# Folding the second layer's attention weights between the steps of the first layer

## The chip, the cores and the metric

The kernel runs on one core of one Trainium2 chip. The metric is the time of one execution on the device in microseconds (us), as the median over runs. All data are 32-bit floats. In the trace every such matmul appears as two instructions ("passes"), and every transpose on TensorE as one.

## The reference

Two layers are computed on x of shape (4, 512, 512). Each adds an attention part and a feed-forward part to x, both computed from the normed rows xn:

```
xn = layernorm(x);  x = x + attn0(xn) + ffn0(xn)
xn = layernorm(x);  x = x + attn1(xn) + ffn1(xn)
```

`attn0` has 32 heads of 16 channels. It walks the 512 tokens in 32 steps of 16; each step uses the state (W1, b1) that the step before left:

```
Z1   = xk @ W1 + b1
grad = backward of a norm at Z1, against the target xv - xk
out  = xq + norm(xq @ W1 - (eta * tril(xq xk^T)) @ grad + b1 - tril(eta) @ grad)
W1   = W1 - (last_eta * xk)^T @ grad;   b1 = b1 - sum(last_eta * grad)
```

Then a norm over the 512 channels and a product with `o_w` follow. `ffn0` is a gated feed-forward with 1408 inner channels.

`attn1` has 16 heads of 128 channels and works from latents, 128 wide for keys and values and 384 for queries:

```
c_kv = xn @ W_DKV + b_DKV;   k = c_kv @ W_UK + b_UK;   v = c_kv @ W_UV + b_UV
c_q  = xn @ W_DQ  + b_DQ;    q = c_q  @ W_UQ + b_UQ
first 64 channels of each head: q <- rope(q @ W_QR), k <- rope(k @ W_KR), the second half of them zero
out  = softmax(q k^T / sqrt(128)) @ v @ W_O + b_O
```

The weights allow two products ahead of any token: a head's columns of W_UK and W_UQ by W_KR and W_QR (the "rotated" columns, 64 per head), and a head's W_UV by its rows of W_O (the "value-output" product, 128 x 512 per head). Since softmax's rows sum to one, the value bias goes to the output as the constant row b_UV @ W_O, which can be added to b_O. `ffn1` has four experts; token i belongs to expert i mod 4.

## The kernel before

**Stages.** Three blocks follow one another in the code: the first layer with the second layer's latents (line 90 on), the second layer's experts (line 822 on), the second layer's attention heads (from about line 928). Each opens memory pools of its own, in SBUF and in PSUM (eight banks).

**The first layer.** Tokens are cut into 8 chunks of 64 per sequence; a chunk has four steps. The loop over n (line 773) emits for each step the state product (`first_product`), the gradient on VectorE (`gradient`), the update of the state, which is kept in PSUM (`update`), and the output (`emit_out`). These depend on each other from step to step. Everything else is "work": a chain of generators, one per chunk (`between`, line 650), that holds the feed-forward (`gate_up` for 11 blocks, `down` for two halves of the rows with 11 weight tiles each), the next chunk's normed and transposed input, its keys, values and queries, and the end of the chunk before (`finish`: norm of the outputs over heads, norm over channels, product with `o_w`, the second layer's layernorm, transposed rows stored to `xe_d`). The last chunk's work ends with `latents`: the products with W_DKV and W_DQ, from rows read back from `xe_d`, stored to `lat_d`.

Each generator yields a number after each piece, its cost in us as the author counts it. `fill(us)` (line 698) adds us to a balance and emits pieces until it is used up. A step calls it three times, with `GAPS` (`LAST_GAPS` in the last chunk): before `update`, before `emit_out`, and after it. A chunk's first step waits in the program until that chunk's inputs are emitted (`done`). After the last step `LAST_FINISH` alternates fills with the pieces of the last `finish`, and what is left follows.

The order on an engine is not exactly this one. When the program is compiled, a list scheduler places the instructions with this order as their priority, and passes over those that it takes not to be ready. The chip then runs each engine's and each DMA queue's instructions in that fixed order. SyncE (SP) issues nearly all loads, in order; ScalarE issues some stores between its own instructions.

**Buffers.** A pool gives each tag so many slots. Those that matter here: `wd` (4 slots, 128 x 512), through which the tiles of the down weights come; `sg` (2); `pn_rs` (1); `xs` (2), through which the latents are stored; `xT` and `q1` (3 each); and in PSUM `pj` (2 banks), which serves nearly every product of the stage other than feed-forward and step (`psum()`, line 102).

**The value bias.** `value_bias(hg)` (line 522) runs in chunks 1 to 4, one head group (4 heads) each. It loads the four heads' rows of W_O as `wd` tiles, multiplies each by its bias spread over 32 columns into one quarter of a PSUM bank, copies the bank, multiplies it by a constant 1/32 to sum it and adds it to `bo`.

**The experts.** Per expert, four pairs of gate and up products (`pg`, `pu`), then four down products (`po`), from one PSUM pool of 2 banks for each of its four tags.

**The heads.** `group_weights(hg)` (line 942) loads a group's weights and folds them. Each 128 x 512 block is transposed per head on TensorE (`turned`, line 933), copied by ScalarE, multiplied by `wkr` or `wqr` and copied over the first 64 channels of each head (`fold`, line 951). Value weights are transposed likewise and multiplied by the output weights into `vo`. Group 0 is folded at the start of the stage, the next one each time sequence 1 of a group begins. A head of a sequence (64 in all) then takes key and query products (`pk`, `pq`), rotation on VectorE and GpSimd, scores (`sc`), softmax on ScalarE and VectorE, a transpose of the probabilities by 16 DMAs from SyncE (`prT`), the context (`pc`) three heads behind, and per four heads the output (`po`).

Of the kernel before, what the change touches and what calls it, by code (L numbers as in the profile page):

```python
# [12 lines left out]
F32 = mybir.dt.float32  # L13
# [23 lines left out]
GAPS, LAST_GAPS = (11.0, 4.0, 8.0), (10.0, 4.0, 5.0)  # L37
LAST_FINISH = (9.0, 17.0, 5.0)
# [17 lines left out]
def trunk_kernel(ctx: ExitStack, tc: tile.TileContext, a: dict, out: bass.AP):  # L56
# [15 lines left out]
    xe_d = dram.tile([2 * NCHUNK, P, NC, E, 32], F32, tag="xe_d", name="xe_d")  # L72
    lat_d = dram.tile([1 + QC // P, P, B, NCHUNK, CT], F32, tag="lat_d", name="lat_d")
# [15 lines left out]
    with ExitStack() as px:  # L89
# [47 lines left out]
        def norm_turn(ch):  # L137
            xTs[ch] = wk.tile([P, NC, CW], F32, tag="xT", name=f"xT{ch}", bufs=3)
            for u in range(2):
                nc.scalar.copy(xTs[ch][:, :, u * P : (u + 1) * P], transposed(xns.pop((ch, u))))  # L140
                yield 0.6
# [96 lines left out]
        def queries(ch):  # L238
            return features(ch, wq_w, q1, "q1", 3)
# [275 lines left out]
        ones32 = one.tile([P, P], F32, tag="ones32", name="ones32")  # L515
        nc.vector.memset(ones32, 1.0 / 32)
        buv16 = one.tile([H, D], F32, tag="buv16", name="buv16")
        nc.gpsimd.dma_start(out=buv16, in_=a["b_UV"].rearrange("(h d) -> h d", d=D))
        buv_b = one.tile([P, H, 32], F32, tag="buv_b", name="buv_b")
        nc.gpsimd.dma_start(out=bo, in_=a["b_O"].unsqueeze(0).to_broadcast([P, HS]))  # L520

        def value_bias(hg):
            if hg == 0:
                pt = psum()[:, :H]
                nc.tensor.transpose(pt, buv16, ident[:H, :H])
                nc.vector.tensor_copy(buv_b, pt.unsqueeze(2).to_broadcast([P, H, 32]))
            pb = psum()
            for h, r in enumerate(quarters):
                w = wk.tile([P, HS], F32, tag="wd", name=f"wob_{hg}_{h}", bufs=4)
                nc.sync.dma_start(out=w, in_=a["W_O"][(4 * hg + h) * D : (4 * hg + h + 1) * D, :])  # L530
                mm(pb[r], buv_b[:, 4 * hg + h, :], w)
            part = wk.tile([P, HS], F32, tag="xt", name=f"bo_part{hg}", bufs=4)
            nc.vector.tensor_copy(part, pb)
            yield 1.3
            pb = psum()
            mm(pb, ones32, part)
            nc.vector.tensor_add(bo, pb, bo)
            yield 0.86
# [7 lines left out]
        def finish(ch):  # L546
# [45 lines left out]
            if ch >= NCHUNK - 2:  # L592
                t = wk.tile([P, NC, CW], F32, tag="xT", name=f"xl_{ch}", bufs=3)
# [56 lines left out]
        def between(ch):  # L650
# [12 lines left out]
            extra = value_bias(ch - 1) if 1 <= ch <= NHG else iter(())  # L663
# [13 lines left out]
            yield from extra  # L677
# [14 lines left out]

        done = {0}
# [83 lines left out]
        for n in range(NM):  # L777
# [8 lines left out]
            update(n, g, pre)  # L786
            fill(gaps[1])
            emit_out(n, po, gh)
            fill(gaps[2])
# [420 lines left out]
```

## Time and profile before

| | |
|---|---|
| median of 3 runs | 2160.28 us (2159.66 to 2162.85) |
| the profiled execution | 2162.4 us |
| its span, first to last instruction | 2160.6 us |
| busy: TensorE, its weight loads | 2068.6 us (96%), 1181.5 us (55%) |
| busy: VectorE, ScalarE, GpSimd | 1177.5, 883.3, 504.9 us |
| first expert matmul, last one ended, first fold of a head group | 1022.4, 1191.9, 1192.75 us |
| matmuls of the folds: transposes, rotations, value-output | 80, 128 and 32 instructions |

How to read it: all times are us from the first instruction of one profiled execution. PE is TensorE, PEld its weight loads, DVE is VectorE, ACT ScalarE, POOL GpSimd, SP SyncE; SPq and ACTq are the DMA issues of those engines. In a row of the timeline, the first number is the start and the second the length of a run of like instructions; in brackets stands the time that the engine was idle before it, and what released it. `out<-in` are tiles by their names in the code. TensorE matmuls overlap, so the distance from start to start tells what one costs, and its listed length is longer.

### The profile page before, as it was taken

The numbers are of one execution on the slowest core, as the hardware profiler recorded it, in microseconds if no ns is written. First come the engines' busy times: TensorE is split into PE (matmuls) and PEld (weight loads), VectorE is DVE, ScalarE is ACT, GpSimd is POOL, SyncE is SP. The second block draws the span as 40 slices with busy tenths as digits, with TensorE's granted clock in tenths as the row PEclk, the third lists the DMA queues.
The fourth block names the chain that finished last, engine by engine and source line by source line (L and its number), as shares of the span: only waits on it lengthen the run. The fifth ranks groups of instructions, "written<-read, shape, count | busy, mean of one in ns | idle before, by whom it ended". The sixth has DMA issues, their size and how long they took to land.

```text
span 2160.6 us, 29279 instructions
## 1 busy us (share of the span) xinstructions
PE 2068.6 (96%) x10050; PEld 1181.5 (55%) x10050; DVE 1177.5 (54%) x2384; ACT 883.3 (41%) x1805; POOL 504.9 (23%) x555
## 2 busy tenths in 40 slices
PE   8999999999999999995999899999999999999998
PEld 6776676767676767543444444444444444444444
DVE  4445656465656565631111556664666656666663
ACT  2334353434434343332000454444544545455552
POOL 4233233233333333301001211110111111111110
PEclk9999999999999999998999989999999999999999
DMA  6556364646474646526610233333233333333332
GB/s 179 153 138 190 112 193 134 180 135 175 131 197 129 173 136 192 171 75 235 226 59 25 89 92 77 74 94 75 76 77 93 75 72 78 75 75 75 95 94 76
DMA packets 286960, 259.27 MB, mean 120 GB/s; under 512 B 52956, under 2 KB 210845, under 8 KB 285789
## 3 DMA queue, kind: packets, MB, share of 16 engines
q1 hardware_dynamic: 272752, 245.96, 41.0%
q10 hardware_dynamic: 11500, 5.32, 0.9%
q0 software_dynamic: 2560, 6.13, 0.8%
q8 instruction: 81, 1.33, 0.3%
q14 instruction: 67, 0.54, 0.1%
HBM read 161.60 MB, written 29.62 MB: 89 GB/s over the span
## 4 chain that ended last, share of the span: by engine, by line
PE 75%; DVE 10%; ACT 9%; DMA 3%; issue 2%; POOL 1%; SPq 0%; ACTq 0%; DVEq 0%; POOLq 0%
PE pj L100 14%; PE pf L100 11%; PE po L1069 10%; PE pc L1054 7%; PE sc L1008 5%; PE pq L999 5%; PE pd L100 5%; ACT prob L1013 3%; PE epg L855 3%; PE epo L900 3%; PE epu L855 3%; ACT prob L1015 2%; PE pso L100 2%; PE pk L992 2%; PE pz L100 2%
## 5 line engine op out<-in xcount | busy, mean ns | idle before, releaser
L1008 PE MATMUL sc<-kT,qT 96*128 96x512 f32 x512 | 235.7, 598 | 15.1 <-ACT prob L1013 13.5
L985 POOL TENSOR_TENSOR kT<-t_k,t_k 32x512 f32<-32x512 f32 x64 | 80.7, 1261 | 717.9 <-PE pq L999 403.3
L1013 ACT ACTIVATE prob<-sc,mx 128x512 f32<-128x512 f32 x256 | 173.1, 683 | 147.1 <-DVE mx L1010 147.1
L1069 PE MATMUL po<-vo,ctxT 128*128 128x512 f32 x512 | 223.0, 593 | 1.5 <-ACT ctxT L1059 1.5
L1054 PE MATMUL pc<-prT,lv 128*128 128x512 f32 x496 | 224.0, 594 | 0.0
L1023 DVE STREAM_TRANSPOSE tt<-prob 128x512 f32<-128x512 f32 x252 | 166.6, 697 | 60.3 <-ACT prob L1015 56.7
L100 PE MATMUL pf<-xT,wg 128*128 128x256 f32 x704 | 171.8, 385 | 4.2 <-DVE hid L459 3.9
L999 PE MATMUL pq<-cq,uq 128*128 128x512 f32 x384 | 175.2, 592 | 0.0
L1015 ACT ACTIVATE prob<-prob,sm 128x512 f32<-128x512 f32 x256 | 171.7, 724 | 3.6 <-DVE sm L1014 3.6
L1008 PEld LDWEIGHTS sc<-kT,qT 96*128 96x128 f32 x512 | 96.0, 191 | 140.9 <-issue 110.6
L100 PE MATMUL pf<-xT,wu 128*128 128x256 f32 x704 | 168.0, 380 | 0.5 <-DMA wu<-in_wu 0.3
L1010 DVE TENSOR_REDUCE mx<-sc 128x1 f32<-128x512 f32 x256 | 164.4, 681 | 7.0 <-PE sc L1008 4.4
L100 PE MATMUL pd<-wd,hid 128*128 128x512 f32 x352 | 165.2, 600 | 0.2
L1069 PEld LDWEIGHTS po<-vo,ctxT 128*128 128x128 f32 x512 | 97.1, 190 | 124.1 <-issue 116.2
L1054 PEld LDWEIGHTS pc<-prT,lv 128*128 128x128 f32 x496 | 94.5, 191 | 120.0 <-issue 112.1
L100 PEld LDWEIGHTS pf<-xT,wg 128*128 128x128 f32 x704 | 131.0, 190 | 32.1 <-DVE hid L459 6.7
L100 PEld LDWEIGHTS pf<-xT,wu 128*128 128x128 f32 x704 | 133.2, 190 | 22.1 <-issue 2.6
L1079 DVE TENSOR_TENSOR y<-po,y 128x512 f32<-128x512 f32 x64 | 44.2, 691 | 152.5 <-PE po L1069 152.5
L993 ACT ACTIVATE kT<-pk,b_UK 64x512 f32<-64x512 f32 x64 | 43.7, 683 | 196.7 <-PE pk L992 196.7
L999 PEld LDWEIGHTS pq<-cq,uq 128*128 128x128 f32 x384 | 73.0, 190 | 91.8 <-issue 86.8
L459 DVE SCALAR_TENSOR_TENSOR hid<-pf,us,sg 128x256 f32<-128x256 f32 x88 | 41.5, 474 | 132.6 <-ACT sg L458 132.0
L297 POOL TENSOR_SCALAR sk<-k,m 128x256 f32<-128x256 f32 x64 | 61.3, 969 | 158.1 <-PE pz L100 158.1
(256 smaller groups left out, 3151.8 us busy)
## 6 DMA issues: line engine op xcount, KB each, us to landing
prT<-tt SPq DMA_DIRECT2D x1008, 64.0 KB, 2.0
wd<-in_wd SPq DMA_DIRECT2D x176, 256.0 KB, 3.0
wg<-in_wg SPq DMA_DIRECT2D x88, 256.0 KB, 3.5
wu<-in_wu SPq DMA_DIRECT2D x88, 256.0 KB, 3.4
rows<-rows SPq DMA_DIRECT2D x128, 66.0 KB, 2.2
kv<-rows SPq DMA_DIRECT2D x32, 264.0 KB, 4.4
gu<-in_gu SPq DMA_DIRECT2D x3, 2048.0 KB, 8.7
xt<-in_x SPq DMA_DIRECT2D x32, 128.0 KB, 3.2
```

The source lines that it names most:

```text
L100: nc.tensor.matmul(out, lhsT=lhsT, rhs=rhs, start=start, stop=stop, skip_group_check=True)
L855: nc.tensor.matmul(ps, lhsT=w[:, c, col : col + P], rhs=xe[:, :, c, e, :], start=(c == 0), stop=(c == NC - 1))
L900: nc.tensor.matmul(po, lhsT=inter[:, i, b * P : (b + 1) * P], rhs=dn[:, i, :], start=(i == 0), stop=(i == EI // P - 1),)
L985: nc.gpsimd.tensor_sub(t[RD:mid, :], t1[RD:mid, :], t2[RD:mid, :])
L999: nc.tensor.matmul(pq, lhsT=w["uq"][i][:, h, :], rhs=cq[:, i, b, :], start=(i == 0), stop=(i == nq - 1))
L1008: nc.tensor.matmul(ps, lhsT=qT[:KQ, i * P : (i + 1) * P], rhs=kT[:KQ, :], start=True, stop=True)
L1010: nc.vector.tensor_reduce(mx, ps, AX.X, ALU.max, negate=True)
L1013: nc.scalar.activation(pr, ps, AF.Exp, bias=mx, scale=1.0, accum_out=sm)
L1015: nc.scalar.mul(pr, pr, sm)
L1023: nc.vector.transpose(out=tt[:, :, :, i, :], in_=pr.rearrange("p (kb e j) -> p kb e j", e=2, j=K))
L1054: ins = nc.tensor.matmul(pc, lhsT=lv[:, b, k, :], rhs=prT[:, k, :], start=(k == 0), stop=(k == E - 1))
L1069: ins = nc.tensor.matmul(po[e], lhsT=ctxT[:, h, e * P : (e + 1) * P], rhs=w["vo"][:, h, :], start=(h == 0), stop=(h == HPG - 1),)
```

## The change

1. The four folds leave `group_weights`. A generator `fold(hg)` in the first layer does them, in ten pieces per head group, chained over the groups. From step 4 on one piece is emitted per step after `update`'s products, and in odd steps another one after `emit_out`'s. A piece loads one 128 x 512 block of weights (`raw`), transposes the block loaded one piece earlier, and multiplies the one turned a piece before that. PSUM is emptied by VectorE for the turned blocks and by ScalarE for the products. ScalarE's DMA queue stores the rotated columns to `rot_d` and the value-output products to `vo_d` in DRAM. Turned blocks and raw blocks have two slots each; the products go through the slots of `sg` and `pn_rs`, the output weights through those of `wd`.
2. `group_weights` loads: for each of W_UK and three blocks of W_UQ the unrotated 64 channels per head from the input and the rotated ones from `rot_d`; and `vo` from `vo_d`.
3. `value_bias` is gone. VectorE adds each head's rows of W_O, times the head's bias as a value per partition, to `bo_part`; one product with the constant 1/512 sums it over the partitions after the last group, and 512 times that is added to `bo`.
4. `GAPS` and `LAST_GAPS` have 22 and 20 us a step instead of 23 and 19; `LAST_FINISH` has six fills of 35 us in all instead of three of 31, one before each piece of the last `finish`. The last chunk's latents then come ahead of work left over.
5. `xT` has 2 slots instead of 3, `q1` 2 instead of 3. The experts' gate and up products get a PSUM pool of their own beside the other one.

```diff
-GAPS, LAST_GAPS = (11.0, 4.0, 8.0), (10.0, 4.0, 5.0)
-LAST_FINISH = (9.0, 17.0, 5.0)
+GAPS, LAST_GAPS = (11.0, 3.0, 8.0), (10.0, 3.0, 7.0)
+FOLDS = CH
+LAST_FINISH = (10.0, 14.0, 7.0, 0.0, 3.0, 1.0)
...
+        def weights_raw(src, nm):
+            raw = wk.tile([P, HPG, P], F32, tag="raw", name=f"raw_{nm}")
+            nc.sync.dma_start(out=raw, in_=src.rearrange("p (h d) -> p h d", h=HPG))
+            return raw
+
+        def weights_turned(raw, nm):
+            pt = psum().rearrange("p (h d) -> p h d", h=HPG)
+            for h in range(HPG):
+                nc.tensor.transpose(pt[:, h, :], raw[:, h, :], ident)
+            t = wk.tile([P, HPG, P], F32, tag="wt", name=f"wt_{nm}")
+            nc.vector.tensor_copy(t, pt)
+            return t
...
-        def value_bias(hg):
+        def fold(hg):
+            c = slice(hg * HPG * D, (hg + 1) * HPG * D)
...
+            srcs = [a["W_UK"][:, c]] + [a["W_UQ"][i * P : (i + 1) * P, c] for i in range(QC // P)] + [a["W_UV"][:, c]]
+            raws, turned, ows = {}, {}, {}
+            for i in range(len(srcs) + 2):
+                if i < len(srcs):
+                    raws[i] = weights_raw(srcs[i], f"{hg}_{i}")
+                if 0 <= i - 1 < len(srcs):
+                    turned[i - 1] = weights_turned(raws.pop(i - 1), f"{hg}_{i - 1}")
+                if i >= 3:
+                    hh = hg * HPG + i - 3
+                    ows[i - 3] = wk.tile([P, HS], F32, tag="wd", name=f"ow_{hh}", bufs=4)
+                    nc.sync.dma_start(out=ows[i - 3], in_=a["W_O"][hh * D : (hh + 1) * D, :])
+                if 0 <= i - 2 < len(srcs) - 1:
+                    wt = turned.pop(i - 2)
+                    pw = psum()[:, : HPG * RD].rearrange("p (h d) -> p h d", h=HPG)
+                    for h in range(HPG):
+                        mm(pw[:, h, :], wt[:, h, :], wr2[:, min(i - 2, 1)])
+                    st = wk.tile([P, CW], F32, tag="sg", name=f"rot_{hg}_{i - 2}")
+                    nc.scalar.copy(st, pw.rearrange("p h d -> p (h d)"))
+                    nc.scalar.dma_start(out=rot_d[hg, i - 2], in_=st.rearrange("p (h d) -> p h d", h=HPG))
+                if i < len(srcs) + 1:
+                    yield 1.9
+            wt = turned.pop(len(srcs) - 1)
+            for h in range(HPG):
+                hh = hg * HPG + h
...
+                ow = ows[h]
+                pv = psum()
+                mm(pv, wt[:, h, :], ow)
+                st = wk.tile([P, HS], F32, tag="pn_rs", name=f"vo_{hh}", bufs=1)
+                nc.scalar.copy(st, pv)
+                nc.scalar.dma_start(out=vo_d[hg, :, h], in_=st)
+                if hh == 0:
+                    nc.vector.tensor_scalar_mul(bo_part, ow, buv[:, :1])
+                else:
+                    nc.vector.scalar_tensor_tensor(bo_part, ow, buv[:, hh : hh + 1], bo_part, ALU.mult, ALU.add)
+                yield 0.9
+            if hg == NHG - 1:
+                pb = psum()
+                mm(pb, onesd, bo_part)
+                nc.vector.scalar_tensor_tensor(bo, pb, float(HS), bo, ALU.mult, ALU.add)
+                yield 0.86
...
             update(n, g, pre)
+            next(folds if FOLDS <= n else iter(()), None)
             fill(gaps[1])
             emit_out(n, po, gh)
+            next(folds if FOLDS <= n and n % 2 else iter(()), None)
             fill(gaps[2])
...
-        for _ in chain(work, fin, latents(NCHUNK - 1)):
+        for _ in chain(latents(NCHUNK - 1), work):
             pass
...
+        ps_gu = px.enter_context(tc.tile_pool(name="d_psgu", bufs=2, space=PSUM))
...
-                pg = psp.tile([P, B * P], F32, tag="pg", name=f"epg_{e}_{i}")
+                pg = ps_gu.tile([P, B * P], F32, tag="pg", name=f"epg_{e}_{i}")
...
-            def loaded(name, src, bufs=2):
-                t = wk.tile([P, HPG, src.shape[-1] // HPG], F32, tag=name, name=f"{name}_{hg}", bufs=bufs)
-                nc.sync.dma_start(out=t, in_=src.rearrange("p (h d) -> p h d", h=HPG))
+            def loaded(name, src, i):
+                t = wk.tile([P, HPG, D], F32, tag=name, name=f"{name}_{hg}")
+                nc.sync.dma_start(out=t[:, :, :RD], in_=src[:, c].rearrange("p (h d) -> p h d", h=HPG)[:, :, :RD])
+                nc.sync.dma_start(out=t[:, :, RD:], in_=rot_d[hg, i])
                 return t
...
+            uk = loaded("uk", a["W_UK"], 0)
+            uq = [loaded(f"uq{i}", a["W_UQ"][i * P : (i + 1) * P], 1 + i) for i in range(QC // P)]
             vo = wk.tile([P, HPG, HS], F32, tag="vo", name=f"vo_{hg}")
+            nc.sync.dma_start(out=vo, in_=vo_d[hg])
```

## The prediction

> **What bounds the kernel now.** I read the totals first, then busy time by stage, then TensorE in order of time where the change takes something away, and last the tail of the first layer.
>
> ```profile
> PE 2068.6 (96%) x10050; PEld 1181.5 (55%) x10050; DVE 1177.5 (54%) x2384; ACT 883.3 (41%) x1805; POOL 504.9 (23%) x555
> ```
>
> TensorE is the only engine near its limit. By stage (columns: stretch, length, busy time of PE, PEld, DVE, ACT, POOL, granted clock, DMA share, GB/s):
>
> ```profile
> 60.00:945.00 885.00, 863.39 (x6903) 618.47 (x6903) 509.87 (x1158) 355.10 (x664) 284.92 (x345) 1.00 0.55 156
> ...
> 962.00:1022.00 60.00, 35.81 (x114) 21.50 (x114) 16.39 (x20) 16.70 (x52) 10.60 (x16) 0.87 0.56 188
> ...
> 1192.00:1210.00 18.00, 13.67 (x61) 9.24 (x62) 0.65 (x1) 6.39 (x13) 1.26 (x1) 0.81 0.36 132
> ...
> 1248.00:1268.00 20.00, 16.70 (x67) 10.69 (x66) 4.19 (x8) 9.79 (x20) 0.00 (x0) 0.74 0.41 98
> 1268.00:2161.00 893.00, 872.64 (x2111) 389.16 (x2109) 561.48 (x1022) 435.60 (x931) 151.18 (x120) 1.00 0.32 80
> ```
>
> The 32 steps (60 to 945) and the attention heads (from 1268) leave TensorE idle 2.4% and 2.3%. The first layer's tail (962 to 1022) leaves it idle 24 us of 60, and the weight folds at 1192 and 1248 run at a clock of 0.81 and 0.74. So work moved from the heads to the steps buys only the difference in how well it is packed; the tail has room.
>
> Here a rule speaks against the reading. The Trainium skill (Perfetto Trace Analysis, Identifying the Most-Contended Engine) calls matmul busy time a bad measure and takes the weight loads' share. That share is 618/885 = 70% in the steps: a quarter of TensorE would be free, the added work would cost nothing there, and the sum below would be 21 us lower. The order of time says otherwise: in the steps 4 down matmuls (8 passes) follow each other in 3.43 us with the next operation at once behind, and idle gaps are rare. I take start-to-start times as occupancy: added work costs its full length.
>
> **What the change takes from the attention stage.** Each head group's fold is 20 transposes, 16 rotations, 4 value-output products, chained through ScalarE copies. TensorE in order of time, first group and then third:
>
> ```profile
> 1192.75 0.63 PE L937 MATMUL ptw_uk<-ident,uk 128*128 128x128 f32 x4 [0.83 <-issue]
> ...
> 1204.43 5.31 PE L970 MATMUL pvo<-ow,wt_uv 128*128 128x512 f32 x8 [0.73 <-ACT wt_uv L939]
> 1209.58 1.02 PE L992 MATMUL pk<-ckv,uk 128*128 128x512 f32 x2
> ...
> 1498.87 3.70 PE L970 MATMUL pvo<-ow,wt_uv 128*128 128x512 f32 x8 [0.67 <-ACT wt_uv L939]
> 1502.40 1.02 PE L992 MATMUL pk<-ckv,uk 128*128 128x512 f32 x2
> ```
>
> From the first transpose to the next key product, less the score passes placed between (4 passes are 1.72): 16.8; 19.2 - 1.7 = 17.5; 16.0 - 3.4 = 12.5 (it begins at 1486.4); again 12.5. Sum 59.4 us. VectorE had little to do at 1248 (4.2 of 20 us): it caught up there on a start at which TensorE waits 1.4 and 4.0 us for scores. Without that pause I give back 2.5 (0 to 8). **-57.**
>
> The loads: weights now come as a half from the input and a half from DRAM, 8 DMAs of 256-byte runs per group, plus one of 1 MB for the products; the 256 KB and 1 MB loads of value and output weights go. SyncE issues 16 DMAs of 0.6 us per head of 13.7 us, so it has 4 us a head to spare. The skill (DMA: Bandwidth & Descriptors, Specifications) puts line rate at runs of 512 B and more, which speaks against this. The rows (KB each, us from issue to landing): 128 KB in 2 KB rows, and 128 KB in 256-byte runs:
>
> ```profile
> xt<-in_x SPq DMA_DIRECT2D x32, 128.0 KB, 3.2
> ...
> z<-zch SPq DMA_DIRECT2D x32, 128.0 KB, 3.1
> ```
>
> No penalty. By the row eight loads are there in 8 x 0.49 issue + 3.1 = 7 us; if short runs took twice as long, in 10. Group 0's are issued at 1178.2 and wanted at 1192.75, so 14.5 us cover either; later groups' are issued hundreds of us ahead. Cost 0 by both.
>
> **What it adds to the steps.** TensorE per group: 20 transposes at 0.11 (4 take 0.43), four rotations of 8 passes at 0.9, 8 passes of products 3.44: 9.2; four groups 37. One column-sum matmul at the end: 0.9. Removed: the bias's matmuls, groups of 13.0 and 4.2 us. **+20.9**, all before the last step.
>
> VectorE gains 20 PSUM copies (0.69) and 16 weighted sums (about 0.7), loses 9 operations of 0.69: +19 us on 510 of 885. ScalarE gains 16 copies of 0.37, 16 of 0.59 and 32 DMA issues of 0.52: +32 on 355. Neither becomes the bound; TensorE's long fills lie over them. DMA: 20 loads of 256 KB, 16 stores of 128 and 16 of 256 KB, 11.5 MB beside some 138: share 0.55 to 0.60.
>
> **Waits added.** (a) Output weights are loaded into the slots of the down weights (four, shared). The planner's costs, added up step by step, place the four output tiles one to three steps before use, and 26 down tiles (8, 7, 11 in the chunks of groups 0 to 2) then find one slot left. A tile with one slot costs issue 0.33 + landing + matmul 0.86:
>
> ```profile
> wd<-in_wd SPq DMA_DIRECT2D x176, 256.0 KB, 3.0
> ```
>
> so 3.3 us of wait each, 87 in all if nothing else runs; behind it on SyncE stand gate weights and the step's key rows. But the trace's TensorE order departs from the program's where an operand is late (gate matmuls stand between down matmuls at 293 to 306), so other ready work goes first, and the ends are 0 and 87. I take 5, near the 8.1 us that all down tiles wait for their loads today. (b) The product store has one buffer: a second product in a step follows a gap of 3 planned us against a store of 2.6 (the latents' 256 KB stores); behind its copy ScalarE holds feature copies and through two PSUM banks TensorE: five pairs, 0 to 15, I take 2. (c) Raw weights through two buffers: 0 to 5, take 1. **+8.** Fewer buffers of normed inputs and queries: the earlier user finishes most of a chunk before; 0.
>
> **The tail.** From the last step's output to the first expert matmul is 76.1 us (946.3 to 1022.4):
>
> ```profile
> 989.66 0.93 ACT L637 ACTIVATE lat<-pj,lat_b 128x64 f32<-128x64 f32 x4 [8.70 <-DMA lat_d<-lat]
> ...
> 993.57 0.98 PE L100 MATMUL pj<-onesd,pn_sq 128*128 128x1 f32 x4 [11.71 <-DVE pn_sq L543]
> ...
> 1022.40 5.88 PE L855 MATMUL epg<-xe,gu 128*128 128x512 f32 x8 [6.74 <-ACT lat L637]
> ```
>
> The planner now leaves four latent pieces of 3.44 us (13.8) for the tail instead of the steps: steps **-13.8**. Counting from the last output: five pieces (17.2) cover the trip through DRAM (16.8); four more run beside the reciprocals, to about +34, as now. The second square, the first line above, no longer stands behind latent copies that wait 8.7 us on their store. But the two PSUM banks still fill with latents whose stores wait for the 2 MB expert load, so I put the row sums at +43.5 rather than +47.3. Then 7.9 output projection, 3.4 + 1.7 latents, 0.9 transposes, 6.9 last latents: +65. The gate products get banks of their own, so the first no longer waits for the last latent copy (6.74 us); its inputs landed at 1013.5 and would land at about +64. So **-11.1**, and without a long gap before it eight passes take 3.43 instead of 5.88: **-2.4**. What is late next is the expert stage's own loads; a layout that puts them over later-freed tiles would eat up to 8.
>
> **Sum.** -57 + 20.9 - 13.8 - 11.1 - 2.4 + 8 = -55.4. The profiled execution took 2162.4 (2160.6 of span and 1.8 around it), so 2107; it stands 2.1 above the runs' median of 2160.3, so 2105.
>
> **The rivals.**
> 1. As summed, within stalls of 0 to 18: 2097 to 2115, named **2105**. Chance 0.55.
> 2. The steps absorb: the folds fall into the 21 idle us between 60 and 945 and added waits are nothing: -8 for the waits, -8 for a third of the idle: **2089**. For it: folds need no step result. Against it: two PSUM banks for all of them. Chance 0.12.
> 3. Partial starvation: slots, banks and late loads cost 18 to 60: **2135**, still faster. For it: 26 tiles with one slot. Chance 0.20.
> 4. The other side: **the down-weight slots decide**. At 87 us (place: down matmuls in steps 8 to 23) the result is 2160.3 - 55.4 - 5 + 87 = **2187**. It decides from 2.5 us of wait per tile (65 of 26 tiles). For it: SyncE issues in order, and the three or four tiles of a down piece need landings of 3.0 us. Against it: 8.1 us of such waits now, and reordering. Chance 0.11.
> 5. The folds were hidden anyway and nothing moves: **2160**. Against it: TensorE's idle in them is bracketed. Chance 0.02.
>
> **How the numbers follow.** Likeliest 2105. A difference of 0.2% (4.3 us) is about what a measurement of this kernel can tell from none. Faster: cases 1 to 3, 0.87; same 0.02; slower 0.11. Below 2085 lies little (rival 2 with no giving back at the start of the heads: 2086); above 2145 lie a third of case 3, which is 0.07, and case 4. Range 2085 to 2145.
>
> **What would show it.** Right: no transposes or value-output products after the expert stage, the first key product within 1 us of the last expert matmul, steps longer by 7 to 15 us, first expert matmul some 65 us after the last step's output without waiting for a latent copy. Wrong: waits of down matmuls for their weights well above 8 us with SyncE standing on output weights; matmuls idle behind product copies; TensorE waiting for scores beyond the first heads; key products waiting for rotated weights.

## The result and the profile after

The changed kernel takes **2178.66 us** (median of 4 runs, 2178.19 to 2180.58), the kernel before in the same session 2161.43. The ratio is 1.0082, 95% interval 1.0064 to 1.0099: slower by some 17 us where 55 us less were forecast. The profiled execution took 2180.6 us, its span is 2178.8 us.

The totals of the page hardly differ:

```profile
PE 2075.2 (95%) x10012; PEld 1183.3 (54%) x10012; DVE 1195.6 (55%) x2412; ACT 860.1 (39%) x1775; POOL 505.6 (23%) x557
```

TensorE is busy 6.6 us longer over a span 18.2 us longer, with 38 instructions fewer. So it isn't work that made the kernel slower; it lost time. Busy time by stage shows where (columns as in the prediction: stretch, length, busy time of PE, PEld, DVE, ACT, POOL, granted clock, DMA share, GB/s):

```profile
60.00:998.00 938.00, 893.96 (x7099) 644.65 (x7099) 529.67 (x1185) 353.31 (x672) 284.50 (x345) 0.98 0.55 159
1015.00:1075.00 60.00, 46.55 (x138) 25.98 (x137) 16.38 (x20) 19.73 (x64) 10.59 (x16) 0.91 0.49 164
...
1270.00:1290.00 20.00, 15.71 (x29) 6.19 (x28) 17.59 (x35) 13.85 (x30) 5.05 (x4) 0.83 0.36 85
1340.00:2178.00 838.00, 823.19 (x1922) 361.72 (x1920) 538.04 (x980) 404.60 (x867) 143.57 (x114) 1.00 0.34 83
```

The steps (first row) now leave TensorE idle 44 of 938 us, against 21.6 of 885 before, and their clock is 0.98, not 1.00. The tail (second row) is filled: 13.5 of 60 us idle instead of 24. At 1270, the new start of the heads, VectorE is busy 17.6 of 20 us while TensorE waits. From 1340 the heads run as before, at 2% idle.

Cut at four events (last output of a step, first expert matmul, first key or fold product of the heads, end), the span divides thus, in us:

| stretch | before | after | difference | forecast |
|---|---|---|---|---|
| to the last step's output | 946.1 | 998.0 | +51.8 | +15.1 |
| tail, to the first expert matmul | 76.3 | 77.7 | +1.4 | -13.5 |
| experts | 170.4 | 176.6 | +6.3 | 0 |
| heads | 967.8 | 926.5 | -41.3 | -57 |
| span | 2160.6 | 2178.8 | +18.2 | -55.4 |

**The steps.** By start-to-start times, TensorE's new work is 42.0 us (products 16.5, rotations 14.7, transposes 9.9, the last sum 1.0). The bias that left was 13.3, the latents that moved to the tail 14.1: +14.6. Idle time adds 22.3. The rest, 15, is put down to the clock: it stood at half for 34.1 us between 60 and 998 (4.2 before), and half of the 29.9 us more is 15. Unchanged work was stretched (gate products from 223 to 232 ns each, up products from 222 to 227, together 10 us). 14.6 + 22.3 + 15 = 52.

What stands behind the idle is seen best at the start of the last chunk. SyncE's issues in order of time:

```profile
882.65 0.38 SPq L280 DMA_DIRECT2D rows<-rows  x1
883.20 0.38 SPq L442 DMA_DIRECT2D zb<-z  x1
883.64 13.30 SPq L280 DMA_DIRECT2D rows<-rows  x7
896.98 0.43 SPq L669 DMA_DIRECT2D W_DQ<-in_W_DQ  x1
900.21 0.34 SPq L293 DMA_DIRECT2D kv<-rows  x1
900.74 0.38 SPq L669 DMA_DIRECT2D W_DQ<-in_W_DQ  x1
901.17 0.50 SPq L457 DMA_DIRECT2D wg<-in_wg  x1
```

and TensorE meanwhile:

```profile
892.16 1.88 PE L103 MATMUL pj<-ow,wt 128*128 128x512 f32 x4
898.32 3.66 PE L103 MATMUL pj<-pn_sq,bones 128*128 128x512 f32 x4 [4.27 <-ACT pn_sq L603]
...
906.09 3.75 PE L103 MATMUL pf<-xT,wg 128*128 128x256 f32 x8 [2.67 <-DMA wg<-in_wg]
```

Seven stores of token rows take 13.3 us to issue. Behind them in SyncE's order stand the gate weights `wg`: they are issued at 901.17 and TensorE waits for them at 906. In the steps as a whole TensorE waits 13.7 us for gate, down and up weights, where it waited 0.6 before, and 8.7 us for the gated activation (3.9 before):

```profile
PE pf L103 <- DVE hid L462: 8.7, 5, 3.7
PE pf L103 <- DMA wg<-in_wg: 5.4, 4, 2.7
PE pd L103 <- DMA wd<-in_wd: 5.3, 9, 1.5
...
PE pf L103 <- DMA wu<-in_wu: 3.0, 3, 2.1
```

The list of SyncE's waits in the steps (waiting line, releaser, us in total, times, longest) says what held it:

```profile
SPq L473 <- PE pj L103: 32.0, 13, 7.6
SPq L473 <- DMA wd<-in_wd: 19.4, 14, 3.3
SPq L280 <- DMA vo_d<-vo: 10.1, 1, 10.1
SPq L457 <- DMA vo_d<-vo: 10.0, 2, 5.6
SPq L457 <- DMA rot_d<-rot: 7.2, 2, 3.7
```

Two things. First, the slots. Down weights (line 473) wait 32 us for products on `pj`. In 22.8 us of this the product is that of an output weight, which has to be used up before its slot is free. The other 9.2 us are row sums of the last norm; they were 4.1 before and stay at 11.6 when the slots are free (e123, below). A further 19.4 us a down weight waits for an earlier one to land; before there was no such wait, and without output weights in these slots (e1_slots) 0.9 us are left.

Second, loads and stores that have nothing to do with the folded weights wait for ScalarE's stores of them (`vo_d`, `rot_d`) to land, 48 us in all with the rows not shown. The semaphores in the trace explain it. Every DMA is counted in on one of a few completion semaphores: the DMAs of SyncE and ScalarE use the same eight, those of GpSimd eight others, and a DMA waits for the one before it on its semaphore. The sixth of the seven row stores, issued at 896.16, shared its semaphore with the store of a product that TensorE made at 892.16:

```profile
893.84 0.33 ACTq L581 DMA_DIRECT2D vo_d<-vo  x1
```

**The tail and the experts.** TensorE and then ScalarE in the tail:

```profile
1046.44 0.61 PE L103 MATMUL pj<-onesd,pn_sq 128*128 128x1 f32 x4 [3.06 <-ACT lat L690]
1051.25 9.14 PE L103 MATMUL pj<-wo,zb 128*128 128x512 f32 x16 [4.20 <-ACT lat L690]
...
1075.64 3.60 PE L910 MATMUL epg<-xe,gu 128*128 128x512 f32 x8
```

```profile
1045.25 1.14 ACT L690 ACTIVATE lat<-pj,lat_b 128x128 f32<-128x128 f32 x4 [5.69 <-DMA lat_d<-lat]
...
1050.27 0.93 ACT L690 ACTIVATE lat<-pj,lat_b 128x64 f32<-128x64 f32 x4 [3.88 <-DMA lat_d<-lat]
```

The first expert matmul no longer waits for a latent copy, as forecast. But the row sums and the output projection do, since the copies wait for buffers whose stores are under way. In the experts one gap is new, in the first of them (TensorE, then VectorE):

```profile
1106.47 5.41 PE L910 MATMUL epu<-xe,gu 128*128 128x512 f32 x8 [6.63 <-DVE inter L949]
```

```profile
1105.27 0.42 DVE L971 TENSOR_SCALAR trig_q<-trig_k 64x512 f32<-64x512 f32 x1 [21.81 <-DMA trig_k<-in_trig]
1105.72 1.29 DVE L949 TENSOR_TENSOR inter<-epu,esg 128x512 f32<-128x512 f32 x2
```

VectorE stands 21.8 us on a small scaling of the rotation table, and the hidden products behind it hold up the two banks of gate and up products. The table's loads are issued from 1094.9 on, behind the expert weights; before they came 12 us after the first expert matmul and VectorE waited 11.0 us for them, now 19 and 21.8. This isn't due to the folds: e5_tail (below), which has none, shows the same stage length, 176.3 us.

### The profile page after: what moved, and what is told of

Its sections match the earlier page's. It is cut to its first block, busy times and chain, and to the rows that moved or that the text cites. A ratio compares the mean times of both kernels' runs of the same rounds, so it can differ in the third digit from the quotient of the medians.

```text
span 2178.8 us, 29272 instructions
## 1 busy us (share of the span) xinstructions
PE 2075.2 (95%) x10012; PEld 1183.3 (54%) x10012; DVE 1195.6 (55%) x2412; ACT 860.1 (39%) x1775; POOL 505.6 (23%) x557
## 4 chain that ended last, share of the span: by engine, by line
PE 68%; DVE 13%; ACT 10%; DMA 6%; issue 2%; POOL 1%; SPq 0%; ACTq 0%; DVEq 0%; POOLq 0%
PE pj L103 13%; PE pf L103 11%; PE po L1099 10%; PE pc L1084 6%; PE pd L103 5%; PE pq L1029 4%; PE sc L1038 4%; ACT prob L1043 4%; ACT prob L1045 3%; PE epo L955 3%; PE epu L910 2%; PE pso L103 2%; DMA wd<-in_wd 2%; PE epg L910 2%; PE pz L103 2%
## 5 line engine op out<-in xcount | busy, mean ns | idle before, releaser
L1038 PE MATMUL sc<-kT,qT 96*128 96x512 f32 x512 | 244.1, 616 | 23.7 <-ACT prob L1043 12.6
L103 PE MATMUL pf<-xT,wg 128*128 128x256 f32 x704 | 178.7, 396 | 16.2 <-DVE hid L462 8.7
L103 PE MATMUL pd<-wd,hid 128*128 128x512 f32 x352 | 172.6, 606 | 5.8 <-DMA wd<-in_wd 5.3
L1029 PE MATMUL pq<-cq,uq 128*128 128x512 f32 x384 | 175.5, 592 | 0.0
```

The source lines that it names most:

```text
L103: nc.tensor.matmul(out, lhsT=lhsT, rhs=rhs, start=start, stop=stop, skip_group_check=True)
L1029: nc.tensor.matmul(pq, lhsT=w["uq"][i][:, h, :], rhs=cq[:, i, b, :], start=(i == 0), stop=(i == nq - 1))
L1038: nc.tensor.matmul(ps, lhsT=qT[:KQ, i * P : (i + 1) * P], rhs=kT[:KQ, :], start=True, stop=True)
```

## The experiments

All were compared with the kernel before on the same chip. The runs were made in five rounds, not all on one chip, in which the kernel before took 2161.43 to 2162.84 us; between rounds the ratios are the fairer measure. Columns: time and ratio with interval, then from the profile the last step's output, the lengths of tail, experts and heads, and TensorE's idle time and time at half clock between 60 us and the last output.

| kernel | us | ratio to before | last output | tail | experts | heads | idle | half clock |
|---|---|---|---|---|---|---|---|---|
| before | 2161.43 | 1 | 946.1 | 76.3 | 170.4 | 967.8 | 21.6 | 4.2 |
| after | 2178.66 | 1.0082 (1.0064 to 1.0099) | 998.0 | 77.7 | 176.6 | 926.5 | 44.0 | 34.1 |
| e1_slots | 2161.59 | 0.9998 (0.9990 to 1.0007) | 977.4 | 76.6 | 176.9 | 928.0 | 37.1 | 18.2 |
| e2_stores | 2175.62 | 1.0070 (1.0055 to 1.0085) | 989.5 | 78.5 | 177.0 | 926.5 | 46.6 | 20.5 |
| e3_tiles | 2173.81 | 1.0060 (1.0045 to 1.0075) | 991.1 | 76.6 | 179.0 | 927.4 | 40.2 | 25.2 |
| e13_no_e2 | 2158.95 | 0.9991 (0.9983 to 0.9999) | 975.9 | 76.4 | 176.8 | 928.0 | 35.1 | 23.9 |
| e17_no_e3 | 2148.70 | 0.9943 (0.9927 to 0.9959) | 966.9 | 77.8 | 179.2 | 927.4 | 26.9 | 13.7 |
| e123 | 2143.33 | 0.9922 (0.9898 to 0.9947) | 955.5 | 76.7 | 177.5 | 928.5 | 21.7 | 3.6 |
| e4_block | 2196.33 | 1.0161 (1.0145 to 1.0176) | 928.6 | 160.7 | 175.5 | 929.0 | 31.7 | 13.7 |
| e5_tail | 2202.65 | 1.0183 (1.0162 to 1.0205) | 977.5 | 78.3 | 176.3 | 968.0 | 59.7 | 44.4 |
| e6_g1 | 2176.31 | 1.0060 (1.0038 to 1.0082) | 995.6 | 78.5 | 176.4 | 928.3 | 42.8 | 31.1 |
| e7_trig | 2147.20 | 0.9921 (0.9902 to 0.9941) | 962.6 | 77.7 | 176.8 | 928.6 | 24.9 | 13.7 |
| e9_lat | 2135.03 | 0.9863 (0.9841 to 0.9886) | 957.7 | 68.8 | 177.7 | 927.6 | 23.1 | 6.8 |
| e10_pool | 2123.78 | 0.9830 (0.9811 to 0.9849) | 959.6 | 67.3 | 168.0 | 926.3 | 23.5 | 7.6 |
| e11_g1 | 2122.42 | 0.9817 (0.9800 to 0.9833) | 959.1 | 67.3 | 168.0 | 926.7 | 29.0 | 17.1 |
| e18_before_lat | 2148.75 | 0.9940 (0.9921 to 0.9959) | 946.9 | 61.0 | 170.2 | 967.7 | 21.9 | 6.8 |
| e19_g1_gaps | 2145.18 | 0.9918 (0.9897 to 0.9939) | 983.1 | 68.6 | 168.0 | 928.1 | 33.9 | 21.1 |

### Which waits make the steps longer

**e1_slots**: output weights in the raw weights' slots, each loaded two products ahead.

```diff
-                    ows[i - 3] = wk.tile([P, HS], F32, tag="wd", name=f"ow_{hh}", bufs=4)
...
+        def out_weights(hh):
+            t = wk.tile([P, HS], F32, tag="raw", name=f"ow_{hh}")
+            nc.sync.dma_start(out=t, in_=a["W_O"][hh * D : (hh + 1) * D, :])
+            return t
```

> The changed kernel, with the output weights loaded into the two slots of the raw weights instead of the four slots of the down weights; the same work and the same bytes. Theory S (slots: the steps are longer because SyncE stands on output weights that hold the down weights' slots, 32 us of such waits, and the weights behind it come late): idle of TensorE on down, gate and up weights falls from 13.7 us to some 5, the half-clock stretches that follow go too, last step's output from 998 to about 983, the whole 2164. Theory C (SyncE's loads wait for ScalarE's stores): under 4 us, 2175 to 2179. Theory P (pieces lengthen the chain of the step, whatever the buffers): no change, 2179.

**e2_stores**: the stores on GpSimd's queue.

```diff
-                    nc.scalar.dma_start(out=rot_d[hg, i - 2], in_=st.rearrange("p (h d) -> p h d", h=HPG))
+                    nc.gpsimd.dma_start(out=rot_d[hg, i - 2], in_=st.rearrange("p (h d) -> p h d", h=HPG))
...
-                nc.scalar.dma_start(out=vo_d[hg, :, h], in_=st)
+                nc.gpsimd.dma_start(out=vo_d[hg, :, h], in_=st)
```

> The changed kernel, with the 32 stores of the folded weights issued by GpSimd instead of ScalarE; the same work and bytes. Theory C (SyncE's loads wait for landings of ScalarE's stores, 48 us of such waits in the steps): those waits vanish, the idle of TensorE on weights falls by half, last output at about 985, the whole 2166. Theory S: no change, 2179. Theory P: no change, or slower by some us where GpSimd's multiplications of the step stand behind a store that waits for its copy.

**e3_tiles**: the products staged in the tile `xs`, which has two slots.

```diff
-                    st = wk.tile([P, CW], F32, tag="sg", name=f"rot_{hg}_{i - 2}")
+                    st = wk.tile([P, CW], F32, tag="xs", name=f"rot_{hg}_{i - 2}")
...
-                st = wk.tile([P, HS], F32, tag="pn_rs", name=f"vo_{hh}", bufs=1)
+                st = wk.tile([P, HS], F32, tag="xs", name=f"vo_{hh}")
```

> The changed kernel, with the folded weights staged for their stores in a two-buffer tile that nothing else uses in the steps but the normed outputs, instead of the tile of the gate activations (rotated weights) and the single one of the last norm's reciprocals (products). Theory T (the shared staging tiles hold up the gate activation and so the hidden product, 8.7 us of idle against 3.9 before, and the second product of a step): last output at about 990, the whole 2170. Theories S, C and P: within 3 us of 2179.

**e123**: all three.

> All three edits at once: output weights in the raw weights' slots, stores from GpSimd, staging in a tile of its own. If waits on buffers and queues are the steps' whole excess (idle 50 against 29 us, and 16 us of lower clock), the last output comes at about 962 and the whole is 2143. If each waits behind another of the same chain, the sum of the three single gains is not reached: 2155 to 2165. Theory P (pieces lengthen the step's own chain): 2170 to 2179.

The slots alone give 17 us, stores and staging tiles alone 3 and 5 (their intervals overlap that of the changed kernel; both had been expected to give more, 13 and 9). In e1_slots TensorE still waits 10.5 us for weights (5 were expected), 8.0 of them at once, and SyncE still waits 40 us for ScalarE's stores. All three give 35, and the steps then look as they did before the change: 21.7 us idle, full clock.

```profile
60.00:955.00 895.00, 873.32 (x7074) 638.19 (x7072) 530.57 (x1187) 353.10 (x670) 306.04 (x377) 1.00 0.56 166
```

The last output comes 9.4 us later than before the change, with 13.7 us of work added on balance (41.1 of new work, less 13.3 and 14.1). So buffers and queues were the steps' whole excess, and no theory in which the pieces lengthen the step's own chain is needed. The single gains don't add up, so two more runs took one edit away from the three; the third pair, stores and tiles with the slots as they were, was not run.

**e13_no_e2** (stores back on ScalarE's queue):

> The changed kernel with two of the three buffer edits: output weights in the raw weights' slots and the separate staging tile, stores still from ScalarE. If SyncE's waits for ScalarE's stores cost by themselves, this stays well above all three together (2143): 2150 to 2160, last output 963 to 972. If the slots and the staging tile are the whole, 2143 to 2147.

**e17_no_e3** (old staging tiles):

> The changed kernel with the output weights in the raw weights' slots and the stores from GpSimd, but staged in the old tiles (that of the gate activations, and the single one of the reciprocals). If slots and stores are the pair that matters (SyncE then stands on neither): 2143 to 2148, last output 955 to 960. If the single staging tile is needed as well, since the products' copies then still wait for each other's stores: 2155 to 2160.

Without the move of the stores 15 us are lost again (by the ratios), though by itself it had gained 3. There SyncE was late anyway: in e2_stores no wait for a store is left, but its waits for products of output weights rose from 22.8 to 28.4 us. The start of e13's last chunk shows the coupling alone (SyncE's issues, its longest wait in that stretch, and TensorE):

```profile
868.85 0.67 SPq L671 DMA_DIRECT2D W_DQ<-in_W_DQ  x1
881.85 0.34 SPq L293 DMA_DIRECT2D kv<-rows  x1
882.38 0.38 SPq L671 DMA_DIRECT2D W_DQ<-in_W_DQ  x1
882.81 0.50 SPq L457 DMA_DIRECT2D wg<-in_wg  x1
```

```profile
SPq L293 <- DMA vo_d<-vo: 12.0, 1, 12.0
```

```profile
886.51 3.75 PE L103 MATMUL pf<-xT,wg 128*128 128x256 f32 x8 [7.56 <-DMA wg<-in_wg]
```

A load of a step's rows waits 12 us for the store of a product, and the gate weights behind it come 7.6 us late. In e123 no wait of SyncE for a store of folded weights is left. e17, with the old tiles, came within 5 us of all three, and the intervals overlap. It lies just above the 2143 to 2148 expected of a pair that carries all, and its last output (966.9) above the 955 to 960. So slots and stores carry most of it, and the tiles perhaps some us. With the stores moved the slots are worth 27 us (e2_stores against e17), not 17.

### What the planner's new numbers do alone

**e5_tail** is the kernel before with the new `GAPS`, `LAST_GAPS`, `LAST_FINISH`, the last pieces' order and the gate products' banks; no early folds.

> The kernel before with the planner's new numbers, the new order of the last pieces and the separate banks of the gate products alone: no weight is folded early, the values' bias stays as it was. By the prediction's sum: last output -13.8 (932), tail 63 instead of 76, the whole 2133. If the tail can't take more than its idle (26 us of idle, of which the moved 13.8 us of latents take half): last output 932, tail 76 to 78, the whole 2146 to 2149. If the smaller gap and later fills starve the steps (the planner's part of the steps' excess): last output above 937, the whole 2152 or more.

The tail came out at 78.3, so the forecast of 63 fails without any fold in play. The steps, though, got 31 us longer while 14 us of work left them. VectorE and then TensorE at the start of a chunk:

```profile
640.15 3.35 DVE L557 RECIPROCAL pn_rs<-pn_rs 128x512 f32<-128x512 f32 x1 [1.60 <-ACT pn_rs L556]
643.53 0.69 DVE L558 TENSOR_TENSOR zb<-zb,pn_rs 128x512 f32<-128x512 f32 x1
645.04 3.35 DVE L557 RECIPROCAL pn_rs<-pn_rs 128x512 f32<-128x512 f32 x1 [0.81 <-ACT pn_rs L556]
...
656.72 0.41 DVE L373 TENSOR_TENSOR grad<-u,rl 128x256 f32<-128x256 f32 x1
```

```profile
658.07 1.08 PE L100 MATMUL wacc<-g_bd,km 128*32 128x64 f32 x32 [10.92 <-ACT g_bd L378]
```

The last norm's two reciprocals and two row norms run in the middle of the step's gradient, and TensorE runs out of other work. That happens at three chunk starts (10.9, 6.7, 8.8 us). In VectorE's order, the kernel before has no such reciprocal between a step's product and its update, e5 has eight, the changed kernel six.

**e4_block**: the changed kernel with all pieces of the folds behind the last step.

```diff
-            next(folds if FOLDS <= n else iter(()), None)
...
-            next(folds if FOLDS <= n and n % 2 else iter(()), None)
...
+        for _ in folds:
+            pass
         fin = finish(NCHUNK - 1)
```

> The changed kernel with all folds in one block behind the last step instead of in pieces between the steps; the planner's numbers as changed. The planner's numbers alone cost the steps 45 us more than they should (idle 60 against 22), so without pieces the same is due here: last output before the block at about 965 to 978, the block 45 to 70 us (its chain runs through copies and loads), the whole 2210 to 2235. If instead the pieces themselves disturb the steps: last output at about 919, the block 45 to 60, the whole 2150 to 2165.

The last output came at 928.6, between the two: the same numbers cost 10 us here, not 45. So they aren't bad by themselves. What differs from e5 is the bias, whose pieces the planner still counts there and which are gone here, and the slots of `xT` and `q1`; which of these shifts the reciprocals was not tried. Six of them stand in the gradient here too, with one gap of 9.3 us. The block took 82 us for some 41 us of work (58 us of the tail at half clock): folded in one go as here, the weights cost twice their work.

**e19_g1_gaps** tried the place of the reciprocals, on a later kernel (e11_g1, below), with a middle gap of 3.4 instead of 3.0:

> The mended kernel with the second group folded in the attention stage, and the planner's middle gap 3.4 instead of 3.0: the last norm's reciprocals then stand between a step's product and its gradient in two steps (three reciprocals) instead of four (six), and no longer in step 28, whose gap of 9 us ate what the missing folds saved. If their place decides: last output 944 to 950, the whole 2108 to 2114. If the steps lack cover anyhow: 2120 to 2126.

It is a miss: the whole became 22 us slower (0.9918 against 0.9817). 10.4 us of latents went back into the steps, but the tail stayed at 68.6 with 20 us at half clock, and the gate weights came late more often (waits before gate products 13 us instead of 7). The place of the reciprocals explains the single long gaps, not the total. How the planner's numbers should stand for the folds stays open.

### The start of the heads

**e6_g1**: the second group folded once more in the attention stage, where it was before, and that result used; the early one is stored but not read.

```diff
-                        ws[hg + 1] = group_weights(hg + 1)
+                        ws[hg + 1] = (folded_here if hg + 1 in HERE else group_weights)(hg + 1)
```

> The changed kernel, with the second group's weights folded a second time in the attention stage, as before the change (the result folded early for that group is not read). Adds 16.7 us of TensorE work behind the fourth head. If the start of the heads is bound by VectorE and the chain of the first scores (TensorE waits for them, 13.5 us of idle and 24 us at half clock up to the first output projection), the fold fills that and costs 0 to 4 us: 2179 to 2183. If the start is bound by TensorE, as the sum in the prediction had it (2.5 us given back), it costs 14 to 17: 2193 to 2196.

Some 17 us of TensorE work more, and the time didn't rise (1.0060, 1.0038 to 1.0082, against 1.0082). The stretch with the fold, after and then e6:

```profile
1250.00:1340.00 90.00, 75.75 (x148) 31.03 (x147) 57.35 (x107) 47.24 (x97) 19.04 (x16) 0.87 0.31 76
```

```profile
1250.00:1340.00 90.00, 82.03 (x208) 38.31 (x209) 55.58 (x102) 50.74 (x104) 18.90 (x15) 0.91 0.28 71
```

TensorE does 60 instructions more in the same 90 us, at a higher clock, while the others do about the same work. The heads as a whole took 1.8 us more. What TensorE waits for there is the chain before the scores; its longest wait in the changed kernel:

```profile
1316.31 3.78 PE L1038 MATMUL sc<-kT,qT 96*128 96x512 f32 x4 [4.63 <-POOL qT L1015]
```

So the second group's fold was nearly free where it stood: TensorE fills with it a start that VectorE and the scores' chain set.

### The experts and the tail

**e7_trig** is e123 with the scaling of the table moved to a later expert in the code.

> The three buffer edits at once, and the scaling of the second trig table moved from the second expert to the third. If the gap of 6.6 us in the second expert (gate and up products wait for the first hidden product, which stands on VectorE behind that scaling, which waits for the trig loads) is what made the expert stage 6 us longer: stage 170 to 171 instead of 177, the whole 2137. If the loads only hold up something else there: no change, 2143.

The stage stayed at 176.8. The edit hadn't done what it said: in the built program the scaling still stood ahead of the hidden products of the first expert (the expectation placed the gap in the second, wrongly):

```profile
1070.22 0.42 DVE L974 TENSOR_SCALAR trig_q<-trig_k 64x512 f32<-64x512 f32 x1 [22.05 <-DMA trig_k<-in_trig]
1070.68 1.29 DVE L951 TENSOR_TENSOR inter<-epu,esg 128x512 f32<-128x512 f32 x2
```

**e9_lat** adds staging tiles for the latents:

```diff
-                st = wk.tile([P, 512], F32, tag="xs", name=f"lat_{ks[0]}_{m}")
+                st = wk.tile([P, 512], F32, tag=("xs", "wt", "raw")[lats[0] % 3], name=f"lat_{ks[0]}_{m}")
```

> As the one before (three buffer edits, trig scaling moved), and the latents staged for their stores in six buffers instead of two. If the tail's two gaps of 3 and 4 us (TensorE waits for latent copies, ScalarE for a buffer whose store stands behind the 2 MB expert load) bound it: tail 69 instead of 77, the whole 2129. If the reciprocals' chain or the expert loads bound it: tail 75 to 77, the whole 2136.

Tail 68.8 instead of 77.7, and the projection's gap shrinks:

```profile
1004.21 7.13 PE L103 MATMUL pj<-wo,zb 128*128 128x512 f32 x16 [0.75 <-ACT lat L693]
```

**e10_pool** gives the scaling to GpSimd:

```diff
-                nc.vector.tensor_scalar_mul(trig_q[RD:, :], trig_k[RD:, :], scale)
+                nc.gpsimd.tensor_scalar_mul(trig_q[RD:, :], trig_k[RD:, :], scale)
```

> The three buffer edits and the six latent buffers, with the scaling of the second trig table given to GpSimd (moving it a line down left it at its place in VectorE's order, ahead of the hidden products of the first expert). If that scaling's wait for the trig loads is what stops VectorE: expert stage 170 to 171 instead of 177, the whole 2129. If something else is late there (the expert loads): stage 174 to 177, the whole 2133 to 2136.

```profile
1057.30 1.49 POOL L974 TENSOR_SCALAR trig_q<-trig_k 64x512 f32<-64x512 f32 x1 [49.27 <-DMA trig_k<-in_trig]
```

GpSimd waits for the table instead, with nothing urgent behind it. The stage falls to 168.0, 2 us below that of the kernel before, and the whole to **2123.78 us**, 0.983 of the kernel before.

**e11_g1** leaves the second group's fold in the attention stage and takes it out of the steps.

> As the one before, and the second group's weights folded in the attention stage as before the change, not in the steps; the other three groups' folds begin six steps later. If the steps are bound by TensorE: last output 9 us earlier (949), heads +2, the whole 7 us below the one before (2122 to 2126). If the planner's smaller gaps need the missing pieces as cover (with the planner's numbers alone the steps stood idle 60 us): last output the same or later, the whole 2130 to 2140.

The whole is the same within the intervals. Of the 9 us that left the steps nothing came back: a gap of 9.1 us opened at the start of the last chunk (the gradient again), and half-clock time rose by 9.5 us. The heads' start gave 5.7 us and the rest of the heads took 6.1.

**What the early folds are worth.** The latents' buffers could have helped the kernel before as well, so **e18_before_lat** has them there (`xs` and `xr` in turn, with the gate products' banks).

> The kernel before with the latents staged in four buffers instead of two, and with the separate banks of the gate products; nothing is folded early. If the latents' stores bound its tail as they did the changed one's (9 us there): tail 66 to 69 instead of 76, the whole 2152. If its tail is bound by the chain of the last norm instead: tail 74 to 77, the whole 2159 to 2162. The early folds are then worth the distance from here to the mended kernel (2124).

It takes 2148.75 us, with a tail of 61.0, less than either case. The mended kernel (e10_pool) is some 24 us below it (0.983 against 0.994 of the kernel before). That is what the early folds bring with all that came with them: the cheaper bias, the planner's numbers, and GpSimd's scaling, which e18 lacks and which left e10's experts 2.2 us shorter. The mends of the tail are worth some 13 us without the folds.

## Why the prediction was wrong

**The size of the waits (+8 forecast, 37 measured: 22 of idle, 15 of clock).** This step decided the sign. Wait (a), output weights in the slots of the down weights, was named with the right mechanism (SyncE stands on one of these tiles, gate weights behind it) and set at 5 of a range of 0 to 87, by the nearest row. e1_slots measures its worth as 17 us. TensorE's own idle on down weights came to 5.3 us, so the 5 fits what was priced; not priced was what stands behind a blocked SyncE (8.4 us on gate and up weights in the changed kernel, not all of it from the slots) and the clock. The row chosen was no measure of that either: its 8.1 us are waits of the weight loads, while TensorE itself waits for no down weight in the kernel before, and there no down weight's load waits for an output weight to be used up. The sign that was named did show in that row (before, then after):

```profile
PEld pd L100 <- DMA wd<-in_wd: 8.1, 17, 1.0
```

```profile
PEld pd L103 <- DMA wd<-in_wd: 22.3, 34, 1.9
```

Waits (b) and (c), set at 3, are not measured one by one; the staging tiles gave 5 (e3_tiles), hardly clear of noise. Rival 4, which decided on wait (a), gave 2187 with 0.11. The measured 2179 is nearest to it, but not by its 87 us: this wait came to a fifth of that, and others that it doesn't have made up the rest.

**A wait that the prediction doesn't have.** ScalarE's stores hold SyncE's loads through shared completion semaphores: 48 us of waits in the changed kernel, worth 15 us once the slots are free (e13_no_e2 against e123). The prediction counted the stores' 0.52 us of issue on ScalarE and their bytes, and asked only who waits behind them on their own engine.

**The clock.** It was counted only where it could bring a gain (-2.4 in the tail). In the steps it cost some 15 us: gaps of 1.7 to 4.3 us were followed by stretches at half clock.

**The work (+20.9 forecast).** The fold's 37.9 measures 41.1 at full clock (in e123), the removed bias 13.3 at TensorE instead of 17.2, since the bracketed time had held other work. So +27.8 would have been right, 7 more (the prediction's own figures add up to 20.7, not 20.9). The latents' -13.8 was right (14.1).

**The tail (-11.1 and -2.4 forecast, +1.4 measured).** The working asked for too much: four pieces of 13.8 us more in the tail and yet 11.1 us less of length, the clock's 2.4 aside, makes 24.9 us out of the 26.3 us of idle between the last output and the first expert matmul. That leaves next to no wait in a chain through norms and DRAM; 13.5 us of idle remained. The chain was laid out by hand without setting the sum against the idle time of the stretch. The part about the gate products' banks was right: the first expert matmul starts at once, eight passes in 3.44 us. The latents' stores were seen as a danger, and held up the tail by 8.9 us (e9_lat).

**The experts (0 forecast, +6.3 measured).** "What is late next is the expert stage's own loads" was right and priced at up to 8; it was then left out of the sum. The waiting instruction was VectorE's scaling, not a product (e10_pool).

**The heads (-57 forecast, -41.3 measured).** The folds' 59.4 us left, and 2.6 us more from the later groups. The giving back at the start was set at 2.5 and measures 20.5: up to the first output projection the heads took 101.8 us before, 34.3 of them in two folds, and take 88.0 now. The kernel before had as much idle and half clock in that stretch (12.5 and 23.9 us; now 13.5 and 23.9), but 6.9 and 17.1 us of it lay inside the folds. So 8 us of idle and 17 us at half clock, worth 8.5, came back outside them, and some 4 us are not accounted for. The rows that showed it stood in the prediction (VectorE catches up at 1248), as did the doubt; the upper end of 8 was too low, since the pause was taken for a help and not for what covered the chain of the first heads. e6_g1 shows the second group's to be nearly free.

**What was right.** Nothing is folded in the heads any more, and their first key product starts 0.8 us after the last expert matmul. No key product waits for rotated weights, so short runs in DRAM cost nothing. The reading that TensorE has no quarter of its time free in the steps held: with these waits gone (e123) the steps take 9.4 us longer for 13.7 us of work added on balance; by the share of weight loads they should have become shorter. That 9.4 is near the sum's +7.1 is in part luck, since the added work was set 7 us too low and some 4 us of it cost nothing.

## What to carry to other kernels

Work put between the steps of a full engine cost no more than its length here only once its loads, stores and staging shared no slot and no completion semaphore with the stream that feeds that engine; list them before counting flops, and price what stands behind each. Check a gain against the idle time of its own stretch, with moved work added: here 25 us were promised out of 26. Work that stands at a stage's start may be cover for the chain behind it; moving it away gains its length less what TensorE then waits.

## What the runs showed of the hardware

Half clock can follow a short pause. In the changed kernel's steps an idle time of 1.75 us before 406.01, with none before it for 10 us, is followed by 3.4 us at half clock from 406.8 on:

```profile
406.01 3.05 PE L103 MATMUL pf<-xT,wg 128*128 128x256 f32 x8 [1.75 <-DMA wg<-in_wg]
```

Eight passes took 2.84 us from start to start there instead of 1.76. The Trainium skill (TensorE: Matmul & The Clock Gate, Why this matters for your kernels) advises to avoid pauses above some 3 us; by that rule this one costs its 1.75 us, by the row 1.1 more in these passes alone. Nor does every such pause bring half clock: one of 1.89 us at 214.9 in the kernel before and two of 2.5 us in e123 (this one, and one at 710.7) did not:

```profile
638.57 1.99 PE L103 MATMUL pf<-xT,wg 128*128 128x256 f32 x8 [2.53 <-DVE hid L462]
```

What decides is not shown here. Every stretch at half clock in the changed kernel's steps was 3.4 us long or twice that.

The same small scaling that held VectorE 21.8 us cost GpSimd 49 us of waiting and the kernel nothing: what an instruction costs is what stands behind it on its engine.
